# First pass of a graph-attention kernel: layer norm of batch 0 in halves, row of sums built twice, adjacency turns moved around the first product

## The chip, the cores and the metric

The kernel runs on one core of a Trainium2 chip. The core's engines are TensorE (PE in the profile), VectorE (DVE), ScalarE (ACT), GpSimd (POOL) and SyncE (SP, which here only issues DMAs). Each engine works through its own instructions in order and waits on semaphores for the others. The metric is the device time of one execution in microseconds, as the median of several runs.

## The reference

Two layers follow each other on 16 batches of 1024 nodes with 256 features (N = 1024, C = 256), all float32. The part that the change touches is the start of layer 0:

```python
h = jnp.maximum(_layernorm(x, axis=-1), 0.0)
x = x + _L0_gnn_ref(h, L0_gnn_para, adj, L0_gnn_kv_w)

# in _L0_gnn_ref, with x standing for h:
fea = jnp.transpose(x, (0, 2, 1))
c_adj = jnp.mean(fea, axis=1)
diff = c_adj[:, None, :] - c_adj[:, :, None]
A = jnp.abs(jnp.abs(jax.nn.sigmoid(diff) - 0.5) - 0.5) * 2.0
A_s = (A + jnp.transpose(A, (0, 2, 1))) * 0.5
Wg = adj[None, :, :] * A_s
g = jnp.einsum('bcn,bnm->bcm', fea, Wg)
g = jax.nn.relu(g * para.reshape(1, C, N))
```

So each node has one number, the mean of its row of h. The graph weight of a pair of nodes is the adjacency entry times a function of the difference of their two means, and the product with h sums over the nodes. The result, scaled by `para`, is the query of an attention with four heads, whose keys and values are products of h with `kv_w`. Layer 1 multiplies the transposed, normalised adjacency with a second layer norm, and puts two linear maps with batch norms behind it.

## The kernel before

**Tiles.** Nodes lie on the 128 partitions in 8 chunks (NC = 8, counted by c). x and h of a batch are tiles of 128 x 8 x 256; each row chunk of the adjacency is its own tile `f_adj` of 128 x 1024. The program is one long list per engine, written out by hand (`manual_schedule`): the order of the calls in the code is the order on each engine.

**Layer norm (class Norm).** `stats` (L219) takes statistics per chunk on DVE (L221) and aggregates them to mean and variance (L223). `invert` (L225) adds epsilon on DVE (L226) and raises to the power -0.5 on POOL (L227). `relu` (L229) makes the shift on DVE (L231) and then h = relu(x * rstd + shift) on ACT, one instruction per chunk (L236), which also sums the chunk's rows of h into `sums`. All of these take the eight chunks at once.

**Row of sums (`prepare_row`, L258).** DVE scales the sums to `col` (L261), one number per node on the partitions. The weights need the same numbers along a row, on every partition. For batches 0 and 1 TensorE builds that with eight transposes of a broadcast column into PSUM (L270), and ACT copies it to `row` (L273); later batches go through DRAM.

**Weights (`weights`, L275).** For chunk c: Abs of the difference on ACT (L279), Tanh on ACT (L282), and on DVE (Tanh - 1) * adjacency (L283).

**The pass (`graph`, L308).** For each chunk it runs the steps that the caller put between the chunks, and then four matrix products of 512 columns, two halves d of the features by two halves g of the nodes (L325), each of which the profile shows as two instructions. They accumulate into two PSUM tiles `f_gps`. At chunk 5 it asks for `para` (L320). Behind the eight chunks come the keys (L343) and their copy (L350), the queries (L352, L353) and the values (L358, L365).

**Work put between.** `turn_adj(i)` (L821) transposes chunk i of the adjacency on TensorE, eight blocks into one PSUM tile (L824), and copies it in a permuted order into `ahatT`, for layer 1 (L825). `turn_h` (L288) makes the transposed h by 32x32 blocks on DVE (L295) and 32 small transfers (L302), which for batch 0 go through SP. `turn_w1` transposes W1 (L874, L896). `make_w1_sums` (L634) adds parts of W1 on DVE and stores them. `row_sums` (L831) sums the adjacency's rows on ACT. `prepare_start(1)` and `prepare_end(1)` are the layer norm of batch 1, in two parts.

**Buffers.** x has one buffer, so batch 1's x can be asked for only when batch 0's has been read, and batch 0's x is loaded again (`again(0)`) once batch 1's has been read. The PSUM pool `ps_s` has three buffers of two banks; two are held by `f_gps` during the pass, and one serves every turn of the adjacency and of W1. The pools `ps_o` and `ps_t` have one bank each and are unused until the attention. The weights share five buffers (`w4`) with W1 and `para`.

**Order before the pass (L877 to L889).** Statistics of batch 0, turns 0 and 1 with copies on ACT, the eight relus, the load of x 1, turns 2 and 3 with copies on DVE, the row of sums, weights of chunk 0, turns 4 and 5, weights of chunk 1. Turns 6 and 7 are in the pass.

Of the kernel before, what the change touches and what calls it, by code (L numbers as in the profile page):

```python
# [10 lines left out]
F32 = mybir.dt.float32  # L11
AF = mybir.ActivationFunctionType
# [5 lines left out]
P = 128  # L18
# [11 lines left out]
def fast_path(  # L30
# [134 lines left out]
    def relu(t, f2):  # L165
        zs[t, f2] = fetch(t, f2)
        relu_on(zs[t, f2], f2)


    with ExitStack() as stage:  # L170
# [9 lines left out]
        st1 = big.tile([P, FC, TT, 6], F32, tag="st1", name="f_st1")  # L180
        bn1.st = st1

        def load_x(b):
            xt = big.tile([P, NC, C], F32, tag="x", name=f"f_x_{b}")
            nc.sync.dma_start(xt, x[b].rearrange("(c p) d -> p c d", p=P))
            return xt


        xs, xr = {0: load_x(0)}, {}

        adj_t = []
        for c in range(NC):
# [13 lines left out]
        class Norm:  # L206


            def __init__(self, xt, name, sums=None):
# [6 lines left out]
                self.h = None  # L216
                self.name = name

            def stats(self, c0, c1):  # L219
                for c in range(c0, c1):  # L220
                    nc.vector.bn_stats(self.st[:, c, :], self.xt[:, c, :])  # L221
                for c in range(c0, c1):
                    nc.vector.bn_aggr(self.mv[:, c, :], self.st[:, c, :])  # L223

            def invert(self):  # L225
                nc.vector.tensor_scalar_add(self.var, self.mv[:, :, 1], EPS)  # L226
                nc.gpsimd.tensor_tensor(self.rstd, self.var, mhalf, ALU.pow)  # L227

            def relu(self, c0, c1):  # L229
                if c0 == 0:  # L230
                    nc.vector.scalar_tensor_tensor(  # L231
                        self.shift, self.mv[:, :, 0], -1.0, self.rstd, ALU.mult, ALU.mult
                    )
                    self.h = two.tile([P, NC, C], F32, tag="h", name=f"f_h_{self.name}")
                for c in range(c0, c1):
                    nc.scalar.activation(  # L236
                        self.h[:, c, :],
                        self.xt[:, c, :],
                        AF.Relu,
                        bias=self.shift[:, c : c + 1],  # L240
                        scale=self.rstd[:, c : c + 1],
                        accum_out=None if self.sums is None else self.sums[:, c : c + 1],
                    )
# [3 lines left out]
        def prepare_start(b):  # L247

            sums_of[b] = small.tile([P, NC], F32, tag="sums", name=f"f_sums_{b}")
            norms[b] = Norm(xs[b], f"a{b}", sums_of[b])  # L250
            norms[b].stats(0, NC)
            norms[b].invert()

        def prepare_end(b):
            norms[b].relu(0, NC)
            hs[b] = norms.pop(b).h

        def prepare_row(b):  # L258

            cols[b] = small.tile([P, NC], F32, tag="col", name=f"f_col_{b}")  # L260
            nc.vector.tensor_scalar_mul(cols[b], sums_of[b], -0.5 / C)  # L261
            row = big.tile([P, N], F32, tag="row", name=f"f_row_{b}")
            rows[b] = row
            if b > 1:
                nc.sync.dma_start(row_d[b].rearrange("(c p) -> p c", p=P), sums_of[b])
                nc.sync.dma_start(row, row_d[b].unsqueeze(0).to_broadcast([P, N]))
                return
            ps = ps_s.tile([P, NC, P], F32, tag="s", name=f"f_rps_{b}")
            for c in range(NC):
                nc.tensor.transpose(  # L270
                    ps[:, c, :], sums_of[b][:, c : c + 1].to_broadcast([P, P]), ident
                )
            nc.scalar.copy(row, ps.rearrange("p c q -> p (c q)"))  # L273

        def weights(b, c):  # L275

# [31 lines left out]
        def graph(b, between):  # L308


            gps = [ps_s.tile([P, N], F32, tag="s", name=f"f_gps_{b}_{d}") for d in range(CC)]
            hT = None
            para_t = []
            for c in range(NC):
                for step in between.get(c, ()):
                    step()
                if c == 5:
                    for d in range(CC):
                        t = w4.tile([P, N], F32, tag="w4", name=f"f_para_{b}_{d}")
# [3 lines left out]
                for d in range(CC):  # L323
                    for g in range(NH):
                        nc.tensor.matmul(  # L325
                            gps[d][:, ts(g, 512)],
                            hs[b][:, c, ts(d, P)],
                            w[:, ts(g, 512)],
                            start=(c == 0),
                            stop=(c == NC - 1),  # L330
                        )
                if c == 0:
                    hT = hTs.pop(b)
            for step in between.get(NC, ()):
                step()
            kT = big.tile([P, CC, N], F32, tag="kT", name=f"f_kT_{b}")
            qT = big.tile([P, CC, N], F32, tag="qT", name=f"f_qT_{b}")
            v = big.tile([P, NC, C], F32, tag="v", name=f"f_v_{b}")
            for d in range(CC):
                ps = ps_s.tile([P, N], F32, tag="s", name=f"f_kps_{b}_{d}")  # L340
                for g in range(NH):
                    for e in range(CC):
                        nc.tensor.matmul(  # L343
                            ps[:, ts(g, 512)],
                            kvw_t[:, e, ts(d, P)],
                            hT[e][:, ts(g, 512)],
                            start=(e == 0),
                            stop=(e == CC - 1),
                        )
                nc.scalar.copy(kT[:, d, :], ps)  # L350

                nc.vector.tensor_mul(qT[:, d, :], gps[d], para_t[d])  # L352
                nc.scalar.activation(qT[:, d, :], qT[:, d, :], AF.Relu, scale=-SCALE)  # L353
            for c4 in range(0, NC, 4):
                ps = ps_s.tile([P, 4, C], F32, tag="s", name=f"f_vps_{b}_{c4}")
                for i in range(4):
                    for e in range(CC):
                        nc.tensor.matmul(  # L358
                            ps[:, i, :],
                            hT[e][:, ts(c4 + i, P)],  # L360
                            kvw_t[:, e, C : 2 * C],
                            start=(e == 0),
                            stop=(e == CC - 1),
                        )
                nc.scalar.copy(v[:, c4 : c4 + 4, :], ps)  # L365
            return qT, kT, v
# [429 lines left out]
        def again(b):  # L796
            xr[b] = load_x(b)
# [20 lines left out]
        dinv = small.tile([P, NC], F32, tag="dinv", name="f_dinv", bufs=1)  # L818
        drow = []

        def turn_adj(i, copy):  # L821
            ps = ps_s.tile([P, NC, P], F32, tag="s", name=f"f_adjps_{i}")
            for m in range(NC):
                nc.tensor.transpose(ps[:, m, :], adj_t[i][:, ts(m, P)], ident)  # L824
            copy(columns(i), ps.rearrange("p m (q i) -> p m i q", i=NC))  # L825

        def unused(name):
            return pp.tile([P, N], F32, tag="p", name=f"f_unused_{name}")
# [46 lines left out]
            return ps.rearrange("p d f q -> p (d f q)")  # L875

        with tc.manual_schedule(engines={ENG.PE, ENG.Activation, ENG.DVE, ENG.Pool, ENG.SP}):  # L877
            prepare_start(0)
            for i in range(2):
                turn_adj(i, nc.scalar.copy)  # L880
            prepare_end(0)
            xs[1] = load_x(1)
            for i in range(2, 4):
                turn_adj(i, nc.vector.tensor_copy)
            prepare_row(0)
            weights(0, 0)
# [8 lines left out]
            def turn_w1():  # L895
# [15 lines left out]
            prepare_row(1)  # L911
            diagonal()
            for b in range(B):
# [965 lines left out]
```

## Time and profile before

| | |
|---|---|
| median of 3 runs | 2459.4 us (2456.1 to 2460.28) |
| the profiled execution | 2456.69 us, of which the span is 2454.9 us |
| busy share of the span | PE 98%, DVE 69%, ACT 54%, POOL 13% |
| PE busy, 0 to 23.1 us | 10.45 us |
| PE busy, 23.1 to 50.9 us | 26.93 of 27.8 us |
| PE busy, 50.9 to 71.0 us | 18.56 of 20.1 us |
| PE busy, 71.0 to 127.0 us | 56.00 of 56.0 us |
| x of batch 0: issue, first use by DVE | 0.74 us, 6.29 us |
| adjacency chunk 0: first use by PE | 8.19 us |
| `f_col` of batch 0 on DVE (L261) | 18.18 us |

The span runs from the first to the last event of the profiled execution; 1.8 us of the time lie around it. All times in the text count from the span's start. A row of the timeline or of the groups gives the start or the count, the length, the engine, the line, the operation, and what it writes and reads; in brackets stands how long the engine was idle ahead of it and what ended that wait.

The bytes that all transfers moved in the first microseconds, from the view of stretches, in GB/s (thousand bytes per us): 20 from 1 to 2 us, 151 from 2 to 3, 342 from 3 to 4, 372 from 4 to 5, 393 from 5 to 6.

### The profile page before, as it was taken

To read this page: it belongs to the slowest core of one execution; us is meant where nothing else is said; L and a number is where in the kernel's file an instruction comes from. 1 tells how busy PE (TensorE), PEld (TensorE's weight loads), DVE (VectorE), ACT (ScalarE), POOL (GpSimd) and SP (SyncE) were. 2 spreads that over 40 slices of the span, in tenths; PEclk is the share of its full clock that TensorE was granted. 3 is DMA by queue.
4 is the path that set the end of the run, shared out by engine and by line. 5 is a ranking of instruction groups with operands and counts; after the bars stand their busy time and mean duration, and the time that the engine had idled before them with its cause. 6 is when DMAs were issued, how large, how long until landed. Compare 5 with 4: busy or idle time off the path is not lost.

```text
span 2454.9 us, 24503 instructions
## 1 busy us (share of the span) xinstructions
PE 2399.2 (98%) x8070; PEld 1060.6 (43%) x8070; DVE 1693.8 (69%) x2309; ACT 1319.9 (54%) x1896; POOL 307.8 (13%) x545
## 2 busy tenths in 40 slices
PE   7999999999999999999999999999999999999995
PEld 4443444434343434444343434343444434434444
DVE  4787668584949486776859494957668586747746
ACT  7746546464636455554546364646546465346643
POOL 2030202020020302020201102030202020000000
PEclk9999999999999999999999999999999999999998
DMA  5041414222331414142323223141414211455569
GB/s 180 5 142 61 146 61 124 82 84 71 113 93 60 139 61 146 60 138 69 115 61 105 81 82 115 64 142 61 146 60 122 84 39 57 134 201 171 170 214 371
DMA packets 174424, 271.81 MB, mean 111 GB/s; under 512 B 37585, under 2 KB 121041, under 8 KB 174289
## 3 DMA queue, kind: packets, MB, share of 16 engines
q1 hardware_dynamic: 154128, 237.62, 30.0%
q0 software_dynamic: 15552, 15.77, 2.5%
q10 hardware_dynamic: 4608, 16.78, 1.7%
q8 instruction: 66, 1.08, 0.2%
q14 instruction: 70, 0.57, 0.1%
HBM read 165.68 MB, written 70.84 MB: 96 GB/s over the span
## 4 chain that ended last, share of the span: by engine, by line
PE 94%; DVE 2%; DMA 2%; ACT 1%; issue 1%; POOL 0%; ACTq 0%; SPq 0%; DVEq 0%; POOLq 0%
PE f_s L379 18%; PE f_o L420 18%; PE f_gps L325 17%; PE f_aps L568 15%; PE f_zps L663 6%; PE f_vps L358 5%; PE f_kps L343 4%; PE f_zx L1092 3%; PE f_zm L1092 2%; PE f_z2ps L1030 2%; DVE f_x1t L1358 1%; PE f_zps L744 1%; PE f_zps3b L663 0%; PE f_zps3a L663 0%; ACT f_h_a L236 0%
## 5 line engine op out<-in xcount | busy, mean ns | idle before, releaser
L387 ACT ACTIVATE f_p<-f_s 128x1024 f32<-128x1024 f32 x512 | 477.4, 1046 | 153.4 <-PE f_s L379 153.2
L396 DVE TENSOR_TENSOR f_acc<-f_acc,f_p 128x1024 f32<-128x1024 f32 x384 | 470.4, 1225 | 42.1 <-DVE f_acc L396 1.4
L379 PE MATMUL f_s<-f_qT,f_kT 64*128 64x512 f32 x2048 | 456.9, 596 | 0.0
L420 PE MATMUL f_o<-f_p,f_v 128*64 128x512 f32 x2048 | 453.6, 595 | 0.0
L325 PE MATMUL f_gps<-f_w,f_h_a 128*128 128x512 f32 x1024 | 444.7, 594 | 3.8 <-DVE f_w L283 3.8
L302 POOL DMA_DIRECT2D f_hT<-f_hQ x480 | 235.7, 499 | 1219.1 <-PE f_gps L325 1088.4
L379 PEld LDWEIGHTS f_s<-f_qT,f_kT 64*128 64x128 f32 x2048 | 190.6, 185 | 263.5 <-ACT f_p L387 117.3
L325 PEld LDWEIGHTS f_gps<-f_w,f_h_a 128*128 128x128 f32 x1024 | 192.8, 190 | 251.9 <-issue 228.6
L420 PEld LDWEIGHTS f_o<-f_p,f_v 128*64 128x64 f32 x2048 | 141.4, 137 | 304.4 <-issue 255.6
L283 DVE SCALAR_TENSOR_TENSOR f_w<-f_w,f_adj 128x1024 f32<-128x1024 f32 x128 | 155.0, 1212 | 52.4 <-ACT f_w L282 52.4
L279 ACT ACTIVATE f_w<-f_row,f_col 128x1024 f32<-128x1024 f32 x128 | 148.2, 1157 | 27.2 <-DMA f_row<-frow 22.6
L236 ACT ACTIVATE f_h_b<-f_x,f_shift_b,f_rstd_b 128x256 f32<-128x256 f32 x128 | 64.6, 587 | 158.5 <-DVE f_shift_b L231 158.5
L611 DVE TENSOR_TENSOR f_aggT<-f_u,f_aps 128x512 f32<-128x512 f32 x16 | 11.0, 687 | 185.5 <-PE f_aps L568 185.5
L282 ACT ACTIVATE f_w<-f_w 128x1024 f32<-128x1024 f32 x128 | 135.4, 1058 | 4.1
L568 PE MATMUL f_aps<-f_ahatT,f_hs 128*128 128x512 f32 x256 | 115.1, 592 | 0.0
L343 PE MATMUL f_kps<-f_hT,f_kvw 128*128 128x512 f32 x256 | 113.2, 593 | 1.5 <-DVE f_qT L352 1.5
L568 PE MATMUL f_aps<-f_t,f_hs 128*128 128x512 f32 x256 | 112.5, 592 | 1.5 <-DVE f_hs L562 1.5
L358 PE MATMUL f_vps<-f_kvw,f_hT 128*128 128x256 f32 x512 | 113.1, 379 | 0.0
L568 PE MATMUL f_aps<-f_ahatT,f_h_b 128*128 128x512 f32 x256 | 112.6, 593 | 0.0
L358 PEld LDWEIGHTS f_vps<-f_kvw,f_hT 128*128 128x128 f32 x512 | 97.3, 190 | 20.1 <-issue 6.2
L236 ACT ACTIVATE f_h_a<-f_x,f_shift_a,f_rstd_a 128x256 f32<-128x256 f32 x128 | 75.0, 587 | 54.4 <-DVE f_shift_a L231 54.4
L393 DVE TENSOR_TENSOR f_acc<-f_p,f_p 128x1024 f32<-128x1024 f32 x64 | 76.2, 1191 | 30.7 <-ACT f_p L387 30.7
(187 smaller groups left out, 2554.7 us busy)
## 6 DMA issues: line engine op xcount, KB each, us to landing
f_t<-ft SPq DMA_DIRECT2D x84, 512.0 KB, 7.6
f_x<-in_x_dram SPq DMA_DIRECT2D x32, 1024.0 KB, 5.6
fz<-f_z SPq DMA_DIRECT2D x64, 512.0 KB, 9.4
f_zb<-fz SPq DMA_DIRECT2D x36, 512.0 KB, 4.2
f_para<-in_L_gnn_para_dram SPq DMA_DIRECT2D x32, 512.0 KB, 4.7
f_att<-f_oT SPq DMA_DIRECT2D x512, 32.0 KB, 1.9
fx<-f_x SPq DMA_DIRECT2D x16, 1024.0 KB, 5.9
f_x1t<-fx SPq DMA_DIRECT2D x32, 512.0 KB, 6.3
```

Source lines behind the costliest of these rows:

```text
L279: nc.scalar.activation(w, rows[b], AF.Abs, bias=cols[b][:, c : c + 1], scale=0.5 / C)
L283: nc.vector.scalar_tensor_tensor(w, w, 1.0, adj_t[c], ALU.subtract, ALU.mult)
L302: queue.dma_start(to[ts(k, 32), ts(a, 32 * NC)], t[ts(a, 32), k].rearrange("i c r -> i (c r)"),)
L325: nc.tensor.matmul(gps[d][:, ts(g, 512)], hs[b][:, c, ts(d, P)], w[:, ts(g, 512)], start=(c == 0), stop=(c == NC - 1),)
L343: nc.tensor.matmul(ps[:, ts(g, 512)], kvw_t[:, e, ts(d, P)], hT[e][:, ts(g, 512)], start=(e == 0), stop=(e == CC - 1),)
L358: nc.tensor.matmul(ps[:, i, :], hT[e][:, ts(c4 + i, P)], kvw_t[:, e, C : 2 * C], start=(e == 0), stop=(e == CC - 1),)
L379: nc.tensor.matmul(ps[:, e, :], kT[rows_e, pair, ts(m, P)], qT[rows_e, pair, ts(g, 512)], start=True, stop=True,)
L387: nc.scalar.activation(p, ps, AF.Exp)
L396: nc.vector.tensor_add(acc_of[s], acc_of[s], p)
L420: nc.tensor.matmul(o_of[s][e * HD : (e + 1) * HD, :], v[:, m, ts(2 * pair + e, HD)], p[:, e, :], start=(m == 0), stop=(m == NC - 1),)
L568: nc.tensor.matmul(ps, left[:, m, :], right(m), start=not more and m == 0, stop=(m == KH - 1), skip_group_check=more,)
L663: nc.tensor.matmul(ps[i], left[:, ts(i, P)], right, start=not more, stop=True, skip_group_check=more,)
```

## The change

Everything lies in the part ahead of the attention of batch 0.

- x of batch 0 is loaded by four transfers of two chunks each in place of one.
- Its layer norm runs in two halves: statistics, power and shifts of chunks 0 to 3, then of 4 to 7. ACT makes h for chunks 0 to 5. DVE makes chunks 6 and 7 with new helpers: subtract the mean and take the maximum with 0, multiply by the inverse deviation, and sum the rows.
- The row of sums of batch 0 is built twice in PSUM. ACT makes chunk 0's weights in two halves straight out of the first, while DVE copies the second to `row`. The products of chunk 0 run by halves of the nodes.
- Ahead of the first product now stand adjacency turns 0, 1 and 2, and 3 to 7 stand in the pass. Turns 2, 4 and 6 go into the two banks of `ps_o` and `ps_t` (`turn_adj_aside`) and are copied in two parts. Copies are all on DVE but that of turn 3.
- The relus of batch 1 and the new load of batch 0's x move from chunk 4 to chunk 6, behind all eight weights; the W1 sums move behind the pass.

```diff
-        def load_x(b):
+        def load_x(b, step=NC):
             xt = big.tile([P, NC, C], F32, tag="x", name=f"f_x_{b}")
-            nc.sync.dma_start(xt, x[b].rearrange("(c p) d -> p c d", p=P))
+            from_x = x[b].rearrange("(c p) d -> p c d", p=P)
+            for c in range(0, NC, step):
+                nc.sync.dma_start(xt[:, c : c + step, :], from_x[:, c : c + step, :])
             return xt
-        xs, xr = {0: load_x(0)}, {}
+        xs, xr = {0: load_x(0, 2)}, {}
...
+            def vector_relu(self, c0, c1):
+
+                self.place()
+                for c in range(c0, c1):
+                    nc.vector.tensor_scalar(
+                        self.h[:, c, :],
+                        self.xt[:, c, :],
+                        self.mv[:, c, 0:1],
+                        0.0,
+                        ALU.subtract,
+                        ALU.max,
+                    )
+
+            def vector_scale(self, c0, c1):
+                for c in range(c0, c1):
+                    nc.vector.tensor_scalar_mul(
+                        self.h[:, c, :], self.h[:, c, :], self.rstd[:, c : c + 1]
+                    )
+                nc.vector.tensor_reduce(
+                    self.sums[:, c0:c1], self.h[:, c0:c1, :], AX.X, ALU.add
+                )
...
-            nc.scalar.copy(row, ps.rearrange("p c q -> p (c q)"))
+            first = ps.rearrange("p c q -> p (c q)")
+            if b > 0:
+                nc.scalar.copy(row, first)
+                return
+
+
+            second = ps_s.tile([P, NC, P], F32, tag="s", name="f_rps2_0")
+            for c in range(NC):
+                nc.tensor.transpose(
+                    second[:, c, :], sums_of[0][:, c : c + 1].to_broadcast([P, P]), ident
+                )
+            w = w4.tile([P, N], F32, tag="w4", name="f_w_0_0")
+            for g in range(NH):
+                at = slice(512 * g, 512 * (g + 1))
+                nc.scalar.activation(
+                    w[:, at], first[:, at], AF.Abs, bias=cols[0][:, 0:1], scale=0.5 / C
+                )
+                nc.scalar.activation(w[:, at], w[:, at], AF.Tanh)
+            nc.vector.tensor_copy(row, second.rearrange("p c q -> p (c q)"))
+            for g in range(NH):
+                at = slice(512 * g, 512 * (g + 1))
+                nc.vector.scalar_tensor_tensor(
+                    w[:, at], w[:, at], 1.0, adj_t[0][:, at], ALU.subtract, ALU.mult
+                )
+            ws[0, 0] = w
...
+                blocks = [(d, g) for d in range(CC) for g in range(NH)]
+                if b == 0 and c == 0:
+                    blocks.sort(key=lambda n: n[1])
...
+        def turn_adj_aside(i):
+
+            turned_adj[i] = [
+                ps_o.tile([P, NC // 2, P], F32, tag="o", name=f"f_adjpsa_{i}"),
+                ps_t.tile([P, NC // 2, P], F32, tag="t", name=f"f_adjpsb_{i}"),
+            ]
+            for m in range(NC):
+                nc.tensor.transpose(
+                    turned_adj[i][m // 4][:, m % 4, :], adj_t[i][:, ts(m, P)], ident
+                )
+
+        def place_adj_aside(i, copy):
+            for n, ps in enumerate(turned_adj.pop(i)):
+                copy(columns(i)[:, 4 * n : 4 * n + 4], ps.rearrange("p m (q i) -> p m i q", i=NC))
...
-            prepare_start(0)
-            for i in range(2):
-                turn_adj(i, nc.scalar.copy)
-            prepare_end(0)
+            BY_VECTOR = 6
+            HALF = NC // 2
+            sums_of[0] = small.tile([P, NC], F32, tag="sums", name="f_sums_0")
+            norm = Norm(xs[0], "a0", sums_of[0])
+            norm.stats(0, HALF)
+            norm.invert(0, HALF)
+            norm.stats(HALF, BY_VECTOR)
+            norm.shifts(0, HALF)
+            norm.stats(BY_VECTOR, NC)
+            norm.invert(HALF, NC)
+            norm.vector_relu(BY_VECTOR, NC)
+            norm.relu(0, HALF, False)
+            norm.shifts(HALF, NC)
+            norm.relu(HALF, BY_VECTOR, False)
+            norm.vector_scale(BY_VECTOR, NC)
+            hs[0] = norm.h
+            turn_adj(0)
+            place_adj(0, nc.vector.tensor_copy)
             xs[1] = load_x(1)
-            for i in range(2, 4):
-                turn_adj(i, nc.vector.tensor_copy)
             prepare_row(0)
-            weights(0, 0)
-            for i in range(4, 6):
-                turn_adj(i, nc.vector.tensor_copy)
             weights(0, 1)
+            turn_adj(1)
+            turn_adj_aside(2)
+            place_adj(1, nc.vector.tensor_copy)
...
-                    1: [lambda: weights(0, 3), lambda: turn_adj(6, nc.scalar.copy)],
-                    2: [turn_w1, lambda: weights(0, 4), lambda: prepare_start(1)],
-                    3: [lambda: weights(0, 5), lambda: turn_adj(7, nc.scalar.copy)],
-                    4: [lambda: weights(0, 6), lambda: prepare_end(1), lambda: again(0)],
-                    5: [lambda: weights(0, 7), make_w1_sums],
+                    1: [
+                        lambda: weights(0, 3),
+                        lambda: place_adj_aside(2, nc.vector.tensor_copy),
+                        lambda: turn_adj(3),
+                        lambda: place_adj(3, nc.scalar.copy),
+                    ],
+                    2: [
+                        lambda: weights(0, 4),
+                        turn_w1,
+                        lambda: prepare_start(1),
+                        lambda: turn_adj_aside(4),
+                        lambda: place_adj_aside(4, nc.vector.tensor_copy),
+                    ],
+                    3: [
+                        lambda: weights(0, 5),
+                        lambda: turn_adj(5),
+                        lambda: place_adj(5, nc.vector.tensor_copy),
+                    ],
+                    4: [
+                        lambda: weights(0, 6),
+                        lambda: weights(0, 7),
+                        lambda: turn_adj_aside(6),
+                        lambda: place_adj_aside(6, nc.vector.tensor_copy),
+                    ],
+                    5: [
+                        lambda: turn_adj(7),
+                        lambda: place_adj(7, nc.vector.tensor_copy),
+                    ],
+                    6: [lambda: prepare_end(1), lambda: again(0)],
...
+            make_w1_sums()
             prepare_row(1)
```

`invert`, `shifts` and `relu` take a range of chunks now; `turn_adj` only transposes, and `place_adj` does the copy.

More of the change, by code (lines that the diff above doesn't have):

```diff
@@ L217, in __init__, with place @@
                 self.name = name
+            def place(self):
+                if self.h is None:
+                    self.h = two.tile([P, NC, C], F32, tag="h", name=f"f_h_{self.name}")
+            def vector_relu(self, c0, c1):
[17 more added lines that the diff above has]
+                )
             def stats(self, c0, c1):
@@ L223, in stats, with invert, shifts, relu @@
                     nc.vector.bn_aggr(self.mv[:, c, :], self.st[:, c, :])
[L225 to L229, printed above, removed]
+            def invert(self, c0=0, c1=NC):
+                at = slice(c0, c1)
+                nc.vector.tensor_scalar_add(self.var[:, at], self.mv[:, at, 1], EPS)
+                nc.gpsimd.tensor_tensor(
+                    self.rstd[:, at], self.var[:, at], mhalf[:, : c1 - c0], ALU.pow
+                )
+            def shifts(self, c0, c1):
+                at = slice(c0, c1)
+                nc.vector.scalar_tensor_tensor(
+                    self.shift[:, at],
+                    self.mv[:, at, 0],
+                    -1.0,
+                    self.rstd[:, at],
+                    ALU.mult,
+                    ALU.mult,
+                )
+            def relu(self, c0, c1, shifts=True):
                 if c0 == 0:
[L231 to L234, printed above, removed]
+                    if shifts:
+                        self.shifts(0, NC)
+                    self.place()
                 for c in range(c0, c1):
@@ L272, in prepare_row @@
                 )
-            nc.scalar.copy(row, ps.rearrange("p c q -> p (c q)"))
+            first = ps.rearrange("p c q -> p (c q)")
[17 more added lines that the diff above has]
+                at = slice(512 * g, 512 * (g + 1))
+                nc.vector.scalar_tensor_tensor(
+                    w[:, at], w[:, at], 1.0, adj_t[0][:, at], ALU.subtract, ALU.mult
+                )
+            ws[0, 0] = w
         def weights(b, c):
@@ L322, in graph @@
                 w = ws.pop((b, c))
[L323 to L331, printed above, removed]
+                blocks = [(d, g) for d in range(CC) for g in range(NH)]
+                if b == 0 and c == 0:
+                    blocks.sort(key=lambda n: n[1])
+                for d, g in blocks:
+                    nc.tensor.matmul(
+                        gps[d][:, ts(g, 512)],
+                        hs[b][:, c, ts(d, P)],
+                        w[:, ts(g, 512)],
+                        start=(c == 0),
+                        stop=(c == NC - 1),
+                    )
                 if c == 0:
@@ L819, in fast_path, with turn_adj @@
         drow = []
-        def turn_adj(i, copy):
+        def turn_adj(i):
             ps = ps_s.tile([P, NC, P], F32, tag="s", name=f"f_adjps_{i}")
@@ L824, in turn_adj, with place_adj @@
                 nc.tensor.transpose(ps[:, m, :], adj_t[i][:, ts(m, P)], ident)
-            copy(columns(i), ps.rearrange("p m (q i) -> p m i q", i=NC))
+            turned_adj[i] = ps
+        turned_adj = {}
+        def place_adj(i, copy):
+            copy(columns(i), turned_adj.pop(i).rearrange("p m (q i) -> p m i q", i=NC))
+        def turn_adj_aside(i):
[6 more added lines that the diff above has]
+                    turned_adj[i][m // 4][:, m % 4, :], adj_t[i][:, ts(m, P)], ident
+                )
+        def place_adj_aside(i, copy):
+            for n, ps in enumerate(turned_adj.pop(i)):
+                copy(columns(i)[:, 4 * n : 4 * n + 4], ps.rearrange("p m (q i) -> p m i q", i=NC))
         def unused(name):
```

## The prediction

> **What bounds the kernel now.** I read first the busy shares with the chain of waits of the whole span, then the chain of the first 72 us, then the timeline by engine there.
>
> ```profile
> PE 2399.2 (98%) x8070; PEld 1060.6 (43%) x8070; DVE 1693.8 (69%) x2309; ACT 1319.9 (54%) x1896; POOL 307.8 (13%) x545
> PE   7999999999999999999999999999999999999995
> PE 94%; DVE 2%; DMA 2%; ACT 1%; issue 1%; POOL 0%; ACTq 0%; SPq 0%; DVEq 0%; POOLq 0%
> ```
>
> TensorE is full everywhere but in the first and last of the 40 slices. The change lies in the first, so nothing after its end need change: the question is when the scores of batch 0 (L379) begin.
>
> ```profile
> 13.37 4.79 ACT f_h_a L236 x16
> ...
> 18.20 0.34 PE f_rps L270
> ...
> 18.56 1.02 ACT f_row L273
> ...
> 19.61 1.16 ACT f_w L279
> 20.79 1.06 ACT f_w L282
> 21.88 1.24 DVE f_w L283
> 23.11 0.04 issue
> 23.16 3.70 PE f_gps L325 x8
> ...
> 52.85 5.34 DMA f_para<-in_L_gnn_para_dram
> ...
> 70.18 0.87 PE f_rps L270 x8
> 71.05 1.05 PE f_s L379 x3
> ```
>
> Up to 23.16 the chain is a line of single steps (columns are start, length, what): eight relus, row of sums, its copy, Abs, Tanh, product with the adjacency. From 23.16 to 71.05 are 47.89 us. The work in it, by distances between starts: 64 product matmuls at 0.43 = 27.5; three turns of eight transposes (two of the adjacency, one of W1) at 0.87 = 2.6; L343 6.88; L358 6.91; L270 0.87: 44.8. So 3.1 us are idle, most of it in two places:
>
> ```profile
> PE f_gps L325 <- DVE f_w L283: 3.8, 2, 2.9
> PE f_kps L343 <- DVE f_qT L352: 1.5, 1, 1.5
> ```
>
> Of the first line's 3.8 us, 2.9 lie ahead of 23.16 and 0.9 ahead of chunk 7 at 50.98, whose weight stood on ACT behind the relus of batch 1. The second is para, landing late.
>
> **The change: from x to the column of sums.** The bytes moved in the stretches of 1 us reach 171 KB at 3.0 us, 513 at 4.0, 885 at 5.0, 1278 at 6.0. The whole x (1049 KB) is thus in at 5.4, and DVE starts at 6.29, 0.9 later. With the same delay the quarters of x are usable at about 4.2, 4.95, 5.6 and 6.3. Bounds: no quarter before 6.3 (+1.7 us at the column of sums, worked out in rival 1), or as stated. I take the second, as the queue's three more issues (0.45 each) end by 2.6.
>
> ```profile
> 6.29 2.71 DVE L221 BATCH_NORM_STATS2 f_st_a<-f_x 128x6 f32<-128x256 f32 x8 [5.23 <-DMA f_x<-in_x_dram]
> 8.91 0.62 DVE L223 BATCH_NORM_AGGREGATE f_mv_a<-f_st_a 128x2 f32<-128x6 f32 x8
> 9.57 0.17 DVE L226 TENSOR_SCALAR f_var_a<-f_mv_a 128x8 f32<-128x8 f32 x1
> ```
>
> Statistics cost 0.33 per chunk, aggregation 0.07. Chunks 0 to 3 end at 5.9, variance at 6.05. POOL issues its six column loads until 6.22, so the first power starts at 6.25. It has four columns: 1.64 for eight (L227) and 0.70 for two (L119) give 0.16 a column, 1.0, so 7.3; shifts end at 7.5. ACT does four relus at 0.59: 9.9. DVE has done chunks 4 and 5 during the power; chunks 6 and 7 stand behind the shifts: 8.3, variance 8.45, second power 8.55 to 9.6. During it DVE runs two subtract-and-max of 256. L1309 shows TENSOR_SCALAR at 806 ns for 1024 and 546 for 512, so some 0.42, 0.35 in a row. The power may be slowed: L227 takes 2.59 us at 39.93 beside DVE products and 1.64 elsewhere. Bounds 0 and 0.95; I take 0.3, the overlap being 0.7 us long. Shifts 10.1. Then ACT's relus 4 and 5 end, with their accumulator read, at 11.45, while DVE scales twice (0.35) and sums 512 (0.65, like two-input 512s): 11.45 too.
>
> [...]
>
> The first adjacency copy now stands before the column of sums on DVE: 1.17 (L825), 12.6; column 12.8. Before it was at 18.35.
>
> **To the first product.** Eight more transposes build the second copy of the row. TensorE is slow early:
>
> ```profile
> 8.19 1.94 PE L824 MATMUL f_adjps<-f_ident,f_adj 128*128 128x128 f32 x8 [8.19 <-DMA f_adj<-in_adj_dram]
> 18.36 1.91 PE L824 MATMUL f_adjps<-f_ident,f_adj 128*128 128x128 f32 x16
> ```
>
> Eight in 1.94, later sixteen in 1.91; the starts change from 0.21 to 0.11 apart at 13.9. Row one ends at 11.9, row two at 13.6 (0.21), turn 1 at 14.7, turn 2 at 15.6 if the pace changes again at 13.9. ACT does Abs and Tanh in halves (0.68 as L686, 0.6 for Tanh, some 0.1 overlapping): 12.85 to 15.35. DVE copies row two 13.65 to 14.8 and multiplies the first half by 15.5. The first product starts at 15.6: **7.6 us earlier**.
>
> [...]
>
> **Inside the pass.** Six turns of the adjacency are done ahead of 23.16 now, three in the new order, so three more lie inside: 3 x 0.87 = **+2.6 us**. Each needs PSUM that a copy frees. ACT's chunk 1 runs 15.35 to 17.55, DVE multiplies to 18.75 and copies turn 1 to 19.9; turn 3 needs that bank, and TensorE, done with chunk 0 at 19.05, waits 0.85. It runs turn 3 to 20.8, chunk 1 to 24.25, W1 to 25.1. DVE: chunk 2 to 21.1, two h transposes (L295) 23.45, chunk 3 24.6, two half copies at 0.62 25.85, which free turn 4's second bank: that turn ends at 26.3 for 25.97, 0.4 lost. So **+1.25 us of new waits**. Then slack grows: turn 6's banks are free at 31.7 (chunk 4 and batch 1's 3.4 us of statistics go first), needed at 34.1; turn 7's at 34.1, needed at 38.4.
>
> Batch 1's relus go behind all eight weights: 0.9 of chunk 7 gone. They begin at 42 on ACT and the row sums behind end at 55, kT's first copy at 56; TensorE asks for that bank at 61. On SP, para no longer follows x for batch 0: h's 32 issues (0.66 each) run 22.4 to 43.6, para lands by 50, as chunk 7 ends (49.6): the 1.5 gone, and with small gaps **-3.1 us of idle**. If h or para came later than 50, each us is paid in full. The W1 sums (4 x 0.35 on DVE, one store) move behind the pass into some 10 us of idle DVE; free. Batch 1's x is asked for at 11.5, behind the adjacency in the queue; free.
>
> From chunk 2 at 26.35: 6 x 3.44 + 3 x 0.87 + 6.88 + 6.91 + 0.87 = 37.9, scores at 64.25. Sum: -7.6 + 2.6 + 1.25 - 3.1 = **-6.8 us**. The profiled run took 2456.69 (span 2454.9 and 1.8 around it): 2449.9. It lies 2.7 under the median, 2459.4; from the median it is 2452.6. I forecast 2452, own range 2448.5 to 2455.
>
> **Rivals.** (1) *The first half gains nothing*: the quarters land together. Statistics 6.3 to 7.6, power to 9.1, shifts 9.3, chunks 6 and 7 10.1, power 11.6, sums 13.15, column 14.5 for 12.8: gain 5.1, 2454.3. For it: one queue, pieces issued within 2 us; against it: bytes flow from 2 us on, in order.
>
> (2) *Half clock at the first product*: transposes stay at 0.21, turn 2 ends at 17.0, and if 5.7 us of products (8.19 to 13.9) must pass, chunk 0 ends at 23.3 and chunk 2 starts 3 us late: gain 3.8, 2455.6, no change that can be told. Against it: the pace above, and 2.9 us of idle ahead of 23.16 did not lower it.
>
> (3) *Slower: DVE sets the pace.* It gets the second row, five whole or halved copies and batch 1's statistics between the products: 25 us of work from 12.8 to 38. It decides once it is 2.5 us late at turn 6; slower by 4.9 needs it about 14 late, say six copies of 3 us in place of 1.2: 2464. Against it: the same layout took 1.17 each at L825.
>
> (4) *The change moves the start, but the pass's end is set by h's transfers*: landing at 45.5, needed at 49.6; an issue of 0.9 for 0.66 adds 3.5: gain 3.3, 2456.1. Against it: the longest of these issues took 1.48, but the median 0.59.
>
> **How the numbers follow.** Forecast 0.60, (1) 0.15, (2) 0.08, (3) 0.07, (4) 0.10. A measurement of this kernel tells about 0.2%, 4.9 us (the runs span 2456.1 to 2460.28). Faster: most of the forecast, half of (1) and a little of (2) and (4): 0.73. Slower (3) and what I do not see: 0.08. Range 2448 to 2457, past (1), (2) and (4), with the scatter of the runs.
>
> **What would show it.** Column of sums at 12.8 (L261's place), first product at 15.6 (beyond 17.5: wrong), 0.21 apart transposes ending near 13.9, a wait of turn 3 on a DVE copy of some 0.9, none of L343 on para, scores at 64.3. It is wrong if scores start after 66, or if the time differs while they do not.

## The result and the profile after

| | before | after |
|---|---|---|
| median of 7 runs each, on the same chip | 2459.4 us (2456.1 to 2460.72) | 2449.17 us (2447.58 to 2450.47) |
| the profiled execution | 2456.69 us, span 2454.9 us | 2449.1 us, span 2447.3 us |
| first scores of batch 0, in the chain of waits | 71.05 us | 64.87 us |

The changed kernel takes 0.996 of the time of the one before (95% interval 0.9951 to 0.997). The scores, from where the two kernels are alike again, begin 6.2 us earlier.

The page of the changed kernel, as far as it answers to the lines shown of before (busy time and share, TensorE in 40 slices, shares of the chain):

```profile
PE 2397.7 (98%) x8078; PEld 1061.2 (43%) x8078; DVE 1701.8 (70%) x2324; ACT 1315.1 (54%) x1890; POOL 307.7 (13%) x546
PE   8999999999999999999999999999999999999995
PE 95%; DVE 2%; DMA 1%; ACT 1%; issue 1%; SPq 0%; POOL 0%; ACTq 0%; DVEq 0%; POOLq 0%
```

Only the first slice moves, from 7 to 8 tenths. The chain of waits of the changed kernel, its first 74 us (start, length, what):

```profile
2.76 6.85 DMA f_adj<-in_adj_dram
...
9.75 1.94 PE f_adjps L891 x8
11.69 1.72 PE f_rps L311 x8
...
13.43 0.69 ACT f_w L328
...
16.02 1.07 ACT f_w L344
...
17.12 1.06 ACT f_w L347
...
19.35 1.23 DVE f_ahatT L897
...
20.62 1.09 PE f_adjps L891 x8
21.71 3.44 PE f_gps L392 x8
...
50.23 6.87 PE f_kps L410 x16
57.09 6.91 PE f_vps L425 x32
64.00 0.87 PE f_rps L311 x8
64.87 7.07 PE f_s L446 x32
```

The start no longer hangs on x and its eight relus. It hangs on the adjacency: TensorE gets chunk 0 at 9.75, and its eight transposes (L891) stand ahead of the first row of sums (L311), so ACT's first Abs starts at 13.43. The chain then follows ACT's weights (L344, L347) and DVE's copy of turn 1 (L897) up to 20.62; from there on it is TensorE without a gap. The waits of TensorE over the same stretch (total us, how often, longest) show what is left:

```profile
PE f_adjps L891 <- DMA f_adj<-in_adj_dram: 9.7, 1, 9.7
PE f_adjps L891 <- DVE f_ahatT L897: 0.3, 1, 0.3
PE f_gps L392 <- DVE f_w L335: 0.3, 1, 0.3
```

Before, its products waited 3.8 us for weights and its keys 1.5 us for the queries. Both waits are gone; the two that came are 0.3 us each. The timeline of the norm in the changed kernel (start, length, engine, line; in brackets the idle time before and what ended it):

```profile
3.94 1.48 DVE L249 BATCH_NORM_STATS2 f_st_a<-f_x 128x6 f32<-128x256 f32 x4 [2.89 <-DMA f_x<-in_x_dram]
...
7.05 0.75 DVE L249 BATCH_NORM_STATS2 f_st_a<-f_x 128x6 f32<-128x256 f32 x2 [1.15 <-DMA f_x<-in_x_dram]
...
9.10 0.61 DVE L229 TENSOR_SCALAR f_h_a<-f_x,f_mv_a 128x256 f32<-128x256 f32 x2
...
9.26 1.05 POOL L256 TENSOR_TENSOR f_rstd_a<-f_var_a,f_mhalf 128x4 f32<-128x4 f32 x1 [1.96 <-DVE f_var_a L255]
...
12.87 0.16 DVE L302 TENSOR_SCALAR f_col<-f_sums 128x8 f32<-128x8 f32 x1
```

The first two quarters of x allow statistics from 3.94, but the third is usable only at 7.05.

Where the 6.2 us come from: the first product starts at 16.64 for 23.16, -6.5; three more turns lie behind it, +2.6; the idle time of TensorE from there to the scores is 0.8 for 3.1, -2.3. (From 16.64 to 64.87 are 48.23 us; the work in them is the 44.8 us of the prediction plus 2.6.) The span is shorter by 7.6; the other 1.4 lie behind the first scores, in code that the change does not touch. From the first scores to the end of the span it is 2383.9 us before and 2382.5 after, and 2382.1 to 2385.9 in the eleven profiles below. That scatter of some 2 us on each side is why a single time does not tell half a microsecond, and why the medians (10.2 us apart here, 7.7 in another comparison of the same two kernels) need not agree with 6.2. So the experiments are read by the start of the scores. In the timeline, used for this from here on, it is 70.98 before and 64.80 after; the chain puts both 0.07 later.

### The profile page after: what moved, and what is told of

Read it like the earlier page. It is cut to its first block, busy times and chain, and to the rows that moved or that the text cites. A ratio compares the mean times of both kernels' runs of the same rounds, so it can differ in the third digit from the quotient of the medians.

```text
span 2447.3 us, 24534 instructions
## 1 busy us (share of the span) xinstructions
PE 2397.7 (98%) x8078; PEld 1061.2 (43%) x8078; DVE 1701.8 (70%) x2324; ACT 1315.1 (54%) x1890; POOL 307.7 (13%) x546
## 4 chain that ended last, share of the span: by engine, by line
PE 95%; DVE 2%; DMA 1%; ACT 1%; issue 1%; SPq 0%; POOL 0%; ACTq 0%; DVEq 0%; POOLq 0%
PE f_s L446 18%; PE f_o L487 18%; PE f_gps L392 18%; PE f_aps L635 15%; PE f_zps L730 6%; PE f_vps L425 5%; PE f_kps L410 4%; PE f_zx L1216 3%; PE f_zm L1216 2%; PE f_z2ps L1154 2%; PE f_zps L811 1%; PE f_zps3b L730 0%; PE f_zps3a L730 0%; DVE f_x1t L1482 0%; PE f_outps L1449 0%
## 5 line engine op out<-in xcount | busy, mean ns | idle before, releaser
L344 ACT ACTIVATE f_w<-f_row,f_col 128x1024 f32<-128x1024 f32 x127 | 147.0, 1158 | 29.1 <-DMA f_row<-frow 28.3
L347 ACT ACTIVATE f_w<-f_w 128x1024 f32<-128x1024 f32 x127 | 134.3, 1058 | 4.0
```

The lines of the kernel that those rows point to most:

```text
L344: nc.scalar.activation(w, rows[b], AF.Abs, bias=cols[b][:, c : c + 1], scale=0.5 / C)
```

## The experiments

Each edits the changed kernel unless it says otherwise. The first four ran on one chip beside 20 runs of the kernel before (median 2457.2 us), the next four on one beside 18 (2458.27), the last three on one beside 22 (2457.48).

### The changed kernel again

No edit; it sets the scatter.

> The changed kernel once more, unedited, as the base of the other three on this chip. If the profile of the change is typical: column of sums at 12.9 us, first product at 16.6, scores of batch 0 at 64.9, each within 0.4 us, and a ratio to the kernel before of 0.996. If the pace change of TensorE (0.21 to 0.11 us between transposes) falls at another moment, the first product moves with it by up to 1 us.

Scores at 64.23 in its profile, 0.57 before those of the first. The adjacency came at 9.39 for 9.75, TensorE's transposes took their faster pace (0.11 us from start to start in place of 0.21) at 12.5 us for 14.0, the first product began at 15.73. Median 2449.48 us, ratio 0.9966 (0.9954 to 0.9978). Differences of less than some 0.6 us between two profiles are not told apart. Losses below are counted from the first profile of the changed kernel; from the second each would be 0.57 more.

### Why the third quarter of x is late: the table load or the four transfers

In the changed kernel the transfers slow down for 1.5 us (119 to 180 GB/s by quarter microseconds from 3.75 to 5.25, 344 to 422 in the kernel before) just when ACT loads its tables (3.99 to 5.27), which stood at 0.74 before. One run moves the table load ahead, the next takes the four transfers back to one.

```diff
         with tc.manual_schedule(engines={ENG.PE, ENG.Activation, ENG.DVE, ENG.Pool, ENG.SP}):
+            nc.scalar.copy(const.tile([P, 1], F32, tag="early", name="f_early"), mhalf[:, 0:1])
             BY_VECTOR = 6
```

> One ACT copy of 128x1 is put first, so that ACT's table load runs at about 1 us and not at 3.99. Theory T: the table load (3.99 to 5.27) is what brought the transfers down to some 140 GB/s from 3.75 to 5.25. Then they stay at 280 or more there, adjacency chunk 0 reaches TensorE at 8.8 in place of 9.75, x's third quarter is used by 6.2 in place of 7.05, the weights' first Abs starts at 12.4 in place of 13.43 and scores at 63.9. Rival G: the dip comes from the four small transfers and the late issue of the adjacency; then the dip stays, chunk 0 comes at 9.7 and scores at 64.9.

```diff
-        xs, xr = {0: load_x(0, 2)}, {}
+        xs, xr = {0: load_x(0)}, {}
```

> x of batch 0 in one transfer again. My theory of the halves: statistics start at 6.3 in place of 3.94, the column of sums stands at 14.4 in place of 12.9, scores at 65.9 (1 us later). Rival: the split only trades x against the adjacency, whose chunk 0 came 1.6 us later; then scores stay within 0.3 of 64.9. On the dip: by T there is one at 6.3 to 7.6 and chunk 0 comes at 9 or later; by G there is none and it comes at 8.2.

The view of stretches, for the microsecond from 4 to 5; the last number is the bytes moved, in GB/s. First the changed kernel, then the early table load, then one transfer:

```profile
4.00:5.00 1.00, 0.00 (x0) 0.00 (x0) 1.00 (x3) 1.00 (x1) 1.00 (x3) 1.00 0.58 136
```

```profile
4.00:5.00 1.00, 0.00 (x0) 0.00 (x0) 1.00 (x5) 0.00 (x0) 1.00 (x3) 1.00 0.78 79
```

```profile
4.00:5.00 1.00, 0.00 (x0) 0.00 (x0) 0.00 (x0) 0.00 (x0) 1.00 (x3) 1.00 1.00 328
```

With the table load at 0.73 the dip is as deep (ACT, the fourth pair, is idle there): 79, then 136 from 5 to 6. With one transfer there is none, 328 and 364, and the table load at 6.51 makes none either (297 from 6 to 7). The dip belongs to the four transfers; the table load falls as its cause. What inside the transfer engines makes it is not shown.

The early table load changed nothing: scores at 64.80, 2450.27 us, ratio 0.9971 (0.996 to 0.9982). With one transfer statistics start at 6.46 and, with halves of the norm on a whole x, the column of sums is at 14.38, the first product at 18.07, scores at 66.23: 1.4 us later. 2452.12 us, ratio 0.9978 (0.9969 to 0.9987). So the split transfers are worth about 1.4 us in spite of the dip.

### The relus of batch 1 and the load of x back into the pass

```diff
                         lambda: weights(0, 6),
+                        lambda: prepare_end(1),
+                        lambda: again(0),
                         lambda: weights(0, 7),
...
-                    6: [lambda: prepare_end(1), lambda: again(0)],
```

> Batch 1's relus and the new load of batch 0's x go back ahead of the weights of chunk 7. If the prediction's two terms belong to this move, 0.9 us of wait ahead of chunk 7 and 1.5 us on para come back: scores at 67.3. Rival: the weights run so far ahead in the new order (done at 33.5, chunk 7 needed at 46.6) and h's transfers end so early that both waits would have gone anyway: scores within 0.4 of 64.9.

The waits of DVE in this run:

```profile
DVE f_qT L419 <- DMA f_para<-in_L_gnn_para_dram: 5.0, 1, 5.0
```

Para is late again, as before the change, and the queries start at 51.16 for 48.55. But TensorE has no wait: chunk 7's weight, at 42.60, is in time, and so are the banks of the keys. Scores at 64.97; 2449.94 us, ratio 0.9971 (0.996 to 0.9983). So undoing this move brings neither of the two waits of before (0.9 and 1.5 us) back.

That does not yet say what took them away, for two other steps of the change are still in this run, and no run takes them out alone. On ACT chunk 4's weights now come ahead of the copy of W1; before, that copy came first, behind 2.95 us of idle, and batch 1's statistics began at 36.40, here at 27.50. And on SP the store of W1's sums no longer stands ahead of para. It waited there for DVE; SP's wait before the change:

```profile
SPq L641 <- DVE f_w1s L640: 1.7, 1, 1.7
```

Para was asked for right behind that store, at 52.85. Asked for 1.7 us earlier, it would have come early enough to spare the wait of 1.5 us; that is an estimate from these rows, not a run.

### All turns but two ahead of the first product

```diff
             place_adj(1, nc.vector.tensor_copy)
+            place_adj_aside(2, nc.vector.tensor_copy)
+            turn_adj(3)
+            turn_adj_aside(4)
+            place_adj(3, nc.vector.tensor_copy)
+            place_adj_aside(4, nc.vector.tensor_copy)
+            turn_adj(5)
+            place_adj(5, nc.vector.tensor_copy)
...
-                        lambda: place_adj_aside(2, nc.vector.tensor_copy),
-                        lambda: turn_adj(3),
-                        lambda: place_adj(3, nc.scalar.copy),
...
-                        lambda: turn_adj_aside(4),
-                        lambda: place_adj_aside(4, nc.vector.tensor_copy),
...
-                        lambda: turn_adj(5),
-                        lambda: place_adj(5, nc.vector.tensor_copy),
```

> Adjacency turns 3, 4 and 5 go back ahead of the first product, with their copies on DVE; 6 and 7 stay in the pass, all else as changed. If moving the turns is what lets the early start count: turn 5 waits for the copy of turn 3, first product at 23.9 in place of 16.6, and TensorE then runs through without waits to scores at 68.7, 3.8 later. Rival: the turns cost the same 0.87 us each wherever they stand, and only the earlier column of sums matters: scores within 1 us of 64.9.

TensorE's timeline in this run:

```profile
15.66 0.60 PE L906 MATMUL f_adjpsb<-f_ident,f_adj 128*128 128x128 f32 x4
...
21.35 1.11 PE L906 MATMUL f_adjpsa<-f_ident,f_adj 128*128 128x128 f32 x4 [4.22 <-DVE f_ahatT L912]
22.26 1.06 PE L906 MATMUL f_adjpsb<-f_ident,f_adj 128*128 128x128 f32 x4
```

Turn 4 stands idle for 4.22 us until DVE has emptied its banks, and after the wait four transposes take 1.1 us in place of 0.60: the pace is halved (in the stretches the granted clock is 0.50 from 21 to 27 us). The first product starts at 24.82, scores at 70.87, 6.1 us later than in the changed kernel: +8.2 at the start, -2.6 for three turns less behind it, +1.2 for products at the low pace, -0.75 of waits that no longer come. I had expected 68.7, without the loss of pace. Behind 24.82 TensorE waits for nothing, though it starts its products later here than before the change. 2454.93 us, ratio 0.9988 (0.9979 to 0.9998). With the turns in this place nearly all of the gain at the scores is lost.

### One row of sums, idle time filled or not, and the kernel before once more

The row is built once and copied by ACT, and chunk 0 gets whole weights:

```diff
-            if b > 0:
+            if True:
                 nc.scalar.copy(row, first)
...
             prepare_row(0)
+            weights(0, 0)
             weights(0, 1)
```

> The row of sums of batch 0 is built once, copied by ACT, and chunk 0's weights are made whole, as in the kernel before; all else as changed. My theory: first product at 17.9 in place of 16.6, but turn 3 waits for DVE's copy of turn 1 in both, and that moves only from 20.6 to 21.3: scores 0.7 later, 65.6. Rival: the gain of the first product is kept to the end: scores 1.2 or more later, 66.1.

Scores came 1.9 us later than in the changed kernel, at 66.74, where I expected 65.6. 2451.4 us, ratio 0.9973 (0.9962 to 0.9985). TensorE's timeline:

```profile
17.79 5.09 PE L392 MATMUL f_gps<-f_w,f_h_a 128*128 128x512 f32 x8 [2.54 <-DVE f_w L348]
```

The first eight products take 5.09 us, behind 2.54 us of idle; in the changed kernel they take 3.67, behind 0.26. The late start itself is 1.15, the pace 1.4, and 0.65 of later waits go. The stretches of TensorE in this run (busy time, then the granted clock, share and rate of the transfers) show the pace as the clock:

```profile
17.00:18.00 1.00, 0.21 (x1) 0.62 0.99 385
18.00:19.00 1.00, 1.00 (x2) 0.50 1.04 377
...
20.00:21.00 1.00, 1.00 (x3) 0.67 1.11 350
```

It is half from 17.24 (a mean of 0.62 is 0.76 us at half) to 20.66, so for 3.42 us, and full on either side. Is it the idle time that costs the pace? The same edit, and turn 2's transposes four times over, which fills the gap with transposes alone:

```diff
-            for m in range(NC):
+            for m in list(range(NC)) * (4 if i == 2 else 1):
                 nc.tensor.transpose(
                     turned_adj[i][m // 4][:, m % 4, :], adj_t[i][:, ts(m, P)], ident
                 )
```

> The row built once, as in the run of that name, with the eight transposes of turn 2 done four times over, so that TensorE is busy where it stood idle for 2.5 us ahead of the first product. Theory: the idle time lets TensorE's pace fall to half, which cost the first eight product instructions 1.4 us (5.09 for 3.67); filled, they take 3.7 and scores stand at 65.3. Rival: the pace does not depend on it, they take 5.1 again and scores stay at 66.7.

```profile
18.06 3.60 PE L392 MATMUL f_gps<-f_w,f_h_a 128*128 128x512 f32 x8
```

The first product starts 0.27 us later than in the run before, and scores are 1.2 us earlier, at 65.52, with eight products in 3.60. 24 transposes whose result is written over again bring the scores nearer. One profile of each would not settle that idle time is the cause, since the same gap can have two outcomes, as the next run shows. Over all thirteen profiles it holds: the first eight products take 3.60 to 3.67 us in the nine with at most 0.26 us of idle right ahead of them, and in three of the four with a gap of 2.5 to 4.2 us the clock falls to half. 2451.17 us, ratio 0.9978 (0.9968 to 0.9988); the times do not tell the two apart. And the kernel before, unedited, profiled once more:

> The kernel before, unedited, for a second profile. If the first profile is typical: first product at 23.2 and scores at 71.0, within 0.4. If the pace change of TensorE or the arrival of the adjacency moves it: up to 1 us away.

```profile
23.11 5.40 PE L325 MATMUL f_gps<-f_w,f_h_a 128*128 128x512 f32 x8 [2.89 <-DVE f_w L283]
```

The same 2.89 us of idle, but now 5.40 us for eight products, where the first profile had 3.70. Its stretches around the loss:

```profile
24.00:25.00 1.00, 1.00 (x3) 0.55 0.37 130
...
27.00:28.00 1.00, 1.00 (x3) 0.74 0.00 0
```

Half clock again for 3.42 us, from 24.10 to 27.52, and so beginning a full microsecond after the products do. In the first profile of before the clock stays at 1.00 there:

```profile
24.00:25.00 1.00, 1.00 (x4) 1.00 0.52 174
```

Scores at 71.76 for 70.98, later by half of the loss, as the keys' wait for the queries is 0.6 us there for 1.5; 2456.04 us for this one run. So the kernel before pays for its idle time in some executions, and in others not.

### x in two transfers, and the next bound

```diff
-        xs, xr = {0: load_x(0, 2)}, {}
+        xs, xr = {0: load_x(0, 4)}, {}
```

> x of batch 0 in two transfers of four chunks. The first power cannot start before 6.24 us, when POOL has issued its column loads, so the first half needs no quarter. If the dip of the transfers comes from the four small ones: it shrinks, the second half is used by 6.4 in place of 7.05, adjacency chunk 0 comes at 8.6 in place of 9.75, the first Abs starts at 12.5 in place of 13.43, scores at 63.9. Rival: two are as bad as four, or the second half lands as late: scores at 64.7 or later.

No such dip (383 GB/s from 4 to 5, though 243 from 5 to 6), the adjacency at 8.55, the faster pace of the transposes at 11.9 us, the first product at 15.24, 1.4 us ahead of the changed kernel. Scores are at 64.26, only 0.54 ahead, which two profiles do not tell apart. The reason is in TensorE's timeline:

```profile
20.08 1.09 PE L891 MATMUL f_adjps<-f_ident,f_adj 128*128 128x128 f32 x8 [1.17 <-DVE f_ahatT L897]
```

What the start gained, turn 3 waits for DVE's copy of turn 1. 2450.57 us, ratio 0.9969 (0.9957 to 0.9981). The same with that copy ahead of chunk 1's weights:

```diff
             prepare_row(0)
-            weights(0, 1)
             turn_adj(1)
-            turn_adj_aside(2)
             place_adj(1, nc.vector.tensor_copy)
+            weights(0, 1)
+            turn_adj_aside(2)
```

> x in two transfers, and DVE copies turn 1 of the adjacency ahead of chunk 1's weights, in the 1.1 us in which it stood idle at 17.1, and not behind them. If turn 3's wait for that bank and the later wait of turn 4 are what holds TensorE after the first product: turn 3 starts at once behind chunk 0 (18.8 in place of 20.62), scores at 62.8, 1.5 under the two transfers alone. Rival: chunk 1's weights or ACT become the next bound and scores stay at 64.0 or later.

The first product starts at 16.23, a microsecond later than in the run before, with the faster pace of the transposes at 13.8 us for 11.9. Turn 3 goes at once behind chunk 0, at 19.74, and the wait is one step further on. DVE's timeline:

```profile
19.92 1.23 DVE L348 SCALAR_TENSOR_TENSOR f_w<-f_w,f_adj 128x1024 f32<-128x1024 f32 x1 [0.90 <-ACT f_w L347]
...
25.06 0.68 DVE L912 COPY f_ahatT<-f_adjpsb 128x512 f32<-128x512 f32 x1
```

DVE waits for ACT's Tanh of chunk 2, so its copies of turn 2 end when they did, and turn 4 starts its second half at 25.79 (25.80 without this edit). Chunk 2 is at 26.28 for 26.29, scores at 64.25. I had expected 62.8. 2450.48 us, ratio 0.9969 (0.9956 to 0.9981). By these rows what bounds the start next is ACT's weights of chunks 1 and 2 with DVE's work behind them; no run found a version that is measurably faster than the change.

### The norm whole again

```diff
-        xs, xr = {0: load_x(0, 2)}, {}
+        xs, xr = {0: load_x(0)}, {}
...
-            norm.stats(0, HALF)
-            norm.invert(0, HALF)
-            norm.stats(HALF, BY_VECTOR)
-            norm.shifts(0, HALF)
-            norm.stats(BY_VECTOR, NC)
-            norm.invert(HALF, NC)
-            norm.vector_relu(BY_VECTOR, NC)
-            norm.relu(0, HALF, False)
-            norm.shifts(HALF, NC)
-            norm.relu(HALF, BY_VECTOR, False)
-            norm.vector_scale(BY_VECTOR, NC)
+            norm.stats(0, NC)
+            norm.invert()
+            norm.relu(0, NC)
```

> x in one transfer, the layer norm of batch 0 whole and all eight relus on ACT, as in the kernel before; the rows, the turns and the rest as changed. Shifts at 11.8, relus to 16.5, column of sums at 16.7, first product at 20.5. If the halves and DVE's share are worth what they move: scores at 68.6, 3.8 later than the change. Rival: a later start lets copies and turns get ahead, and less than 2 us of it reach the scores: 66.8 or earlier.

The chain of waits of this run:

```profile
0.74 5.57 DMA f_x<-in_x_dram
...
9.87 1.69 POOL f_rstd_a L256
...
11.78 4.79 ACT f_h_a L277 x16
...
16.61 0.48 PE f_rps L311
17.09 1.71 PE f_rps L322 x8
```

It is the chain of before again, with the relus from 11.78 (13.37 before, behind two copies on ACT). First product at 21.21, scores at 68.96 for the 68.6 expected; 2456.02 us, ratio 0.9994 (0.9985 to 1.0004). Halves, split transfers and DVE's share of h together are worth 4.2 us, 1.4 of it by the transfers. Part of the 4.2 is pace: here the transposes became faster only at 20.4 us, and the first product came 4.6 us later than in the changed kernel where the column of sums came 3.7 later (16.59).

So, each part taken out alone: place of the turns 6.1, norm 4.2, second row 1.9, relus and para 0.2 (within the scatter). They add up to 12.4, twice the gain. Of that 2.6 us are pace that two of the variants lost and the first profile of before did not (1.2 and 1.4). The rest is not traced; a variant can stall where neither kernel does, like the 4.22 us with the turns ahead.

## Why the prediction was right, step by step

The forecast of 2452 us stood 2.8 over the median. Scores were put at 64.25 in the chain and came at 64.87, in the second profile of the same kernel 0.57 earlier. The gain to the scores was put at 6.8 and was 6.2: right in size, by steps of which several were not, so that part of the agreement is luck.

**x to the column of sums.** "The quarters of x are usable at about 4.2, 4.95, 5.6 and 6.3": the first came at 3.94, the third at 7.05. The flow of bytes was taken from one large transfer, and four small ones did not keep it (136 GB/s from 4 to 5 us for 372). Rival 1, that the quarters land together, was half right, for the second half of x. It cost little: the first power had begun by 6.24 and took 1.06 (1.0 predicted), ACT's relus ran at 0.59, and the column of sums was at 12.87 for 12.8.

**The power beside DVE.** The 0.3 us taken for a slowdown did not come: 1.05 us with two subtract-and-max beside it, 1.06 with DVE idle for all but the last 0.25 of it, and these two took 0.61, as did the two scalings behind the power at 10.43.

**To the first product.** 15.6 predicted, 16.64 measured, 15.73 in the second profile. The step that failed is an unspoken one: "row one ends at 11.9" takes for granted that the adjacency arrives as before, at 8.19. With four transfers ahead of it in the queue it came at 9.75, turn 0 held TensorE to 11.5, and row one ended at 13.4. All seven profiles with four transfers have it between 9.2 and 9.9; the four with one or two have it between 8.2 and 8.6. The change of pace, read as 13.9 in the trace of before, stands at 14.4 there; in the changed kernel it came at 14.0. Of the 7.6 us put to the start 6.5 came.

**Turns.** Three more in the pass at 0.87, as predicted; turn 3 waits for DVE's copy of turn 1, at 20.62 rather than 19.95, for 0.3 us rather than 0.85, since the late start ate the difference. The new waits and gaps come to 0.8 rather than 1.25. A late start and a short wait offset each other; the run with two transfers shows both, an early start and a wait of 1.17. That is why a microsecond at the start is worth half of one or less in these profiles: up to chunk 2 DVE and ACT set the pace, as rival 3 had it, but only for the first 10 us of the pass, and by far less than would make the kernel slower.

**The idle time gone.** The 3.1 us went, as predicted, but not for the reason given. "0.9 of chunk 7 gone" was put to the relus' new place and "the 1.5 gone" to para's. With both put back nothing came back on TensorE, so that move is not needed. The earlier start is not needed either: with the turns ahead, where relus and para keep their new place, the first product came at 24.82, later than before the change, and no wait followed it. One of the two may still be enough without the other. Besides them stand two steps that no run takes out, chunk 4's weights ahead of W1's copy and the store of W1's sums, which the prediction called free though it had held para for 1.7 us. The sum was right, the attribution wrong or unproven, and which step does it stays open.

**Pace.** Rival 2, half pace at the first product, did not come, since the change leaves only 0.26 us of idle there. But the ground given against it, "2.9 us of idle ahead of 23.16 did not lower it", held for one execution of two. No run shows the 5.7 us of products that it lets pass first: in all thirteen profiles the transposes go from 0.21 to 0.11 us apart before any product has run, and behind 24 more of them the first eight products took 3.60 us for 5.09.

**h and para.** Rival 4 did not come: TensorE's keys wait for nothing, and with para 5.0 us late on DVE they still do not.

**From the profile to the median.** The profile of before lay 2.7 us below its median of 3, which I added to the forecast. The profile of after lay on its median, 2449.1 for 2449.17. Over 20, 18 and 22 more runs the kernel before has medians of 2457.2 to 2458.27, 0.5 to 1.6 above its profiled time: the three runs shown were high, and 2 us of scatter behind the first scores is more than the steps miss by.

## What to carry to other kernels

Where a start is a chain of single steps, shorten it and then ask which engine feeds the pass behind it: here 1.4 us at the first product were worth at most some 0.5 at the scores, no more than the scatter, since copies and weights on DVE and ACT set the next starts. When one transfer is cut into several, time the transfer behind it in the queue as well, since that one may become the first operand that is late. Put moved work where TensorE would stand idle, even a few us ahead of its first long run of products: the gap costs its length, and in three of four profiles here the pace after it too (a granted clock of 0.50).

## What the runs showed of the chip

- **Transfers.** Four transfers of 256 KB in a row, ahead of those of the adjacency, moved 79 to 146 GB/s from 4 to 5 us in five profiles (the changed kernel's two, and the runs with the early table load, the turns ahead and the row built once); one of 1 MB or two of 512 KB moved 328 to 383 in the same microsecond in four (the two of before, and the runs with one transfer and with two).
- **TensorE's clock.** Idle times of 2.54, 2.89 and 4.22 us were followed by a granted clock of 0.50, and another 2.89 was not. It stayed low for 3.42, 3.42 and 6.84 us (20.42 to 27.26 in the run with the turns ahead, by the means of its stretches, 0.71 and 0.87), so for one or two equal lengths, and once began only after work had come back. At the end of the span the clock changed at 2410.54, 2413.95, 2420.78, 2431.02 and 2448.09 us in the first profile of before and at 2403.35, 2410.18, 2417.01, 2423.83 and 2440.90 in the first of the changed kernel: 3.41 us apart, or two, three or five times that. Why one gap of 2.89 us was followed by half the clock and the other was not is not shown.
- **The early pace.** Up to a moment between 11.9 and 20.4 us in the thirteen profiles transposes start 0.21 us apart, later 0.11, yet the view gives the granted clock as 1.00 in those early stretches too: the first record of the clock starts only at that change (14.38 us in the first profile of before, 14.02 in the first of the changed kernel). There the pace must be read from the distances between instructions.
- **Table load.** In the changed kernel ACT's table load starts at 3.99 us, once x has come, which the first activation reads; before, ahead of the copy of an adjacency turn, it started at 0.74, long before that turn was done (10.16). Moved to 0.73 it gained nothing, since ACT was idle.
